# Attention scores evicted two heads at a time, block maxima joined by a TensorE transposition, and a new written-out order

## The chip, the core and the metric

The kernel runs on one core of one Trainium2 chip. The metric is device time in microseconds (us) from start to end of one launch; lower is better. The engines are named as the profile names them: PE (TensorE, with PEld for its weight loads), DVE (VectorE), ACT (ScalarE), POOL (GpSimd) and SP (SyncE, which issues the DMAs). All arithmetic is in fp32.

## The reference

One transformer block with cross-attention: 8 sequences of 256 tokens, a context of 256 tokens for each, width 512, 16 heads of 32, hidden width 2048.

```python
x = layer_norm(hidden_states, ln1_w, ln1_b)
q = x @ q_w + q_b;  k = enc @ k_w + k_b;  v = enc @ v_w + v_b      # 16 heads of 32
scores = einsum('bhqd,bhkd->bhqk', q, k) * scale
scores = where(mask, scores, finfo.min)
attn = softmax(scores, axis=-1)
out = einsum('bhqk,bhkd->bhqd', attn, v) @ cproj_w + cproj_b
hidden = out + residual
y = layer_norm(hidden, ln2_w, ln2_b)
y = gelu(y @ fc_w + fc_b, approximate=True) @ proj_w + proj_b
return hidden + y
```

## The kernel before

**Staging.** The batch is cut into two groups of four sequences. For each group the kernel makes q, k and v, then attention, then the output projection with the second layer norm, then the MLP (`fc`, gelu, `proj`). All large products are made block-wise with seven products in place of eight (`quad`, L848), in the MLP twice nested; the sums and differences of blocks that this needs are made by DVE and POOL. Products of each `quad` go to three PSUM banks X, Y and W.

**Attention.** `attention` (L1384) walks over 32 units. A unit `ghb` is group g, a set hg of four heads, and sequence b: unit 023 is group 0, heads 8 to 11, sequence 3. `scores` (L1009) does the following for a unit:

- `s`: eight matmuls make the transposed scores, keys on the partitions (two halves kc of 128 keys) and 256 queries along the row, for four heads j. A head's contraction is 32 deep, so four matmuls, one for each head, run in the four row strips of the array at once ("32\*128" in the profile). Each head has a PSUM bank of its own.
- `ev` (L1018, by the helper at L619): ACT copies them to SBUF tiles `pr` and adds the mask as a bias for each partition: eight instructions of 128x256.
- `mx` (L1022): two DVE instructions transpose blocks of 32x32 and take the maximum of each block row, over the keys of one strip of 32 partitions. `mt` (L1026) turns the result, three ACT copies `mc` (L1029) bring strips 1 to 3 to the partitions of strip 0, and `fold` (L1030) takes the maximum over eight blocks.
- `md` and `mm`: the 32x32 result goes to DRAM and comes back as one row of 1024 maxima, laid out on all 128 partitions.
- `less` (L1047 on POOL in two instructions, L1042 on DVE in one): subtracts them, and `exp` (L1050) follows on ACT.

`attend` (L1057) then makes the sums of the exponentials and the product with v, 16 matmuls with 32 columns each in four column strips ("128\*32"), divides on DVE (`r` at L1073 to L1076) and writes the head outputs (`att`, by the helper at L630).

**Order.** Nothing is scheduled at build time. Every step is recorded as a named operation (`T.op`), and `Order.run` (L94) puts them out in the order of the words of `PROGRAM`; a letter behind a colon picks the engine where there is a choice (V for DVE, A for ACT, G for POOL). Each engine works through its own instructions in that order and waits at semaphores where it needs another engine. `PLACES` gives each tile its slot; in PSUM there are three banks W and five banks C.

```python
BANKS = {"W": 3, "C": 5}
...
sb = [Buf(f"s{u}_{j}", "C", 2) for j in range(4)]
```

Of the kernel before, what the change touches and what calls it, by code (L numbers as in the profile page):

```python
# [43 lines left out]
class Order:  # L44
# [49 lines left out]
    def run(self):  # L94
# [20 lines left out]
        for o in order:  # L115
            for b in o.bufs:
                if b.slot is None and b.name in where:
                    w = where[b.name]
                    b.home = w[0] if not w[0].isdigit() else b.kind
                    b.slot = int(w.lstrip("WC"))  # L120
# [4 lines left out]
cq0_00_1 cq0_00_0 vw00 cq0_01_1 cq0_01_0 rows8 rows7 cq0_10_0 turn_c0_00 rows0 turn_c0_10 c0_00:A cq0_10_1 c0_10:V  # L125
cq0_11_0 small v0_0_P1 cq0_11_1 kw01 turn_c0_11 fw0_01_0 v0_1_P1 c0_11:A vw11 rows5 turn_c0_01 rows2 turn_c0_30
vw10 c0_01:A turn_c0_20 mk c0_30:A c0t1:G c0_20:V v0_0_t1:A vw01 turn_c0_21 v0_1_t1:V turn_c0_31 fw0_11_1 k0_0_P2
c0_21:V rows3 c0_31:V c0t2:V kw10 k0_1_P2 rows4 kw11 c0t3:V kw00 rows6 v0_0_P2 vws1:V fw0_10_0 c0t4:V fw0_00_0
v0_1_P2 vws2:V fw0_00_1 kws1:V xt0_3 rows1 k0_1_P1 fw0_10_1 kws2:V mk~1 xt0_0 kws3:V fw0_11_0 v0_0_c11 fw0i1_1:G
v0_1_P6 fw1_00_1 vws4:V xt0_2 fw0i1_2:V fw0s3:V fw1_00_0 k0_0_P1 v0_1_t2:A xt0_6 fw0i7_1:V fw1_10_0 v0_1_c11  # L130
fw0i7_2:G fw1_11_0 cols v0_1_P5 cols~1 qw10 k0_0_t1:V qw11 fw0i7_4:V fw0s1:V xt0_1 v0_0_P6 v0_1_t3:A fw1_11_1
fw0s2:V fw1_10_1 xt0_5 k0_0_P6 fw0i6_3:V xt0_4 k0_1_t1:V fw0i6_1:G cb fw0i5_1:G v0_1_P3 k0_0_t2:V kws4:G fw0i1_4:V
k0_1_P6 stats_x0_30 fw0i1_3:G fw1i1_1:V stats_x0_00 fw0i6_2:G k0_0_P5 fw1i1_3:V k0_1_t2:A xt0_7 v0_0_t2:V fw1i1_2:G
fw0_01_1 stats_x0_10 fw1i1_4:G fcd0_1_True aggr_x0_30 k0_1_P5 fw1i4_1:V qw01 aggr_x0_00 stats_x0_01 fw1i4_2:G
fw1_01_0 fw0i6_4:V fcd0_6_False stats_x0_11 k0_1_P7 k0_1_t3:A fw1_01_1 aggr_x0_01 fw0i7_3:V k0_0_t3:A eps_x0_0
fcd0_7_False stats_x0_31 pow_x0_0 qw00 aggr_x0_31 k0_1_P3 fw1i4_4:G k0_1_c22 fcd0_7_True fw0i5_2:G aggr_x0_11
fcd0_5_False nb_x0_0 k0_0_c11 fw0i5_4:G norm_x0_01:A v0_0_P5 aggr_x0_10 k0_1_c11 fw0i2_1:G norm_x0_00:A fw1i4_3:V
k0_1_c12:A fw0i2_2:V k0_0_P7 eps_x0_1 eps_x0_3 fw0i5_3:V stats_x0_20 pow_x0_3 stats_x0_21 pow_x0_1 k0_0_P3 nb_x0_3
nb_x0_1 fw0i2_3:V norm_x0_31:A aggr_x0_20 aggr_x0_21 eps_x0_2 fw0i2_4:V norm_x0_10:A pow_x0_2 k0_0_c22 fcd0_2_True
k0_1_P4 v0_0_t3:V fw1i2_1:G fcd1_4_True k0_0_c12:A fcd0_6_True norm_x0_11:A nb_x0_2 fw0s4:V kd0_0_11 k0_0_P4  # L140
fcd1_1_True vws3:V norm_x0_20:A fcd0_3_False fw1i2_2:V fcd0_5_True norm_x0_21:A qws1:V turn_x0_10 norm_x0_30:A
fw1i2_4:G k0_0_c21 turn_x0_00 x0_10:A turn_x0_20 turn_x0_30 x0_20:A v0_0_P3 x0_30:V qws3:G xt1_2 cb1_02 x0_00:V
v0_1_c12:A fw0i3_1:V turn_x0_31 fw1i2_3:V turn_x0_11 fw0i3_2:V x0_31:A turn_x0_21 fw1s1:V turn_x0_01 q0_0_P1
x0_01:A qws2:G v0_0_c12:V fcd1_5_False x0_21:A k0_1_c21 fcd1_2_True fw1i5_3:G cb1_20 x0_11:A q0_0_P2 cb1_03
q0_0_t1:A x0t1:V q0_1_P1 fw0i3_3:V q0_0_c11 x0t2:V s000 fw0i3_4:V x0t3:V q0_0_P6 ev000_11 ev000_31 fw1s3:V xt1_3
ev000_10 ev000_01 cb1_12 q0_0_P7 x0t4:V kd0_0_21 q0_0_t2:A fcd1_7_False q0_1_t1:A fw1s2:V ev000_21 ev000_00 q0_0_P5
mx000_0 fw1s4:G fcd1_6_False cb1_10 q0_1_P6 q0_0_t3:A ev000_30 q0_0_c22 ev000_20 stats_x1_10 fcd1_3_False q0_1_P2
fw1i3_3:V fw1i5_1:V q0_1_t2:V fw1i5_2:G mx000_1 q0_0_P4 fw1i6_1:G qws4:G q0_1_c11 q0_1_P5 q0_0_c21 fw1i5_4:V mt000
fw0i4_3:G fcd1_5_True mc000_3 mc000_2 s020 cb1_13 mc000_1 fw1i6_3:G fold000 cb1_00 fw1i7_1:V q0_0_P3 md000 ev020_30
fw0i4_1:V ev020_21 fw1i7_2:V cb1_23 ev020_00 fw0i4_2:G cb1_21 ev020_10 fw1i7_4:G ev020_20 cb1_01 q0_1_P7 ev020_01  # L150
cb1_11 fw1i3_1:G ev020_31 q0_0_c12:A mx020_1 fw1i6_2:G ev020_11 s002 fw1i3_2:G mm000 mx020_0 fw0i4_4:G v0_1_P7
fw1i7_3:G mt020 stats_x1_11 mc020_2 mc020_3 fw1i6_4:G q0_1_t3:V ev002_30 ev002_11 fw1i3_4:G aggr_x1_10 aggr_x1_11
v0_0_P7 mc020_1 q0_1_c22 ev002_01 ev002_00 fold020 ev002_10 eps_x1_1 md020 ev002_31 pow_x1_1 ev002_20 q0_1_P3
fcd1_7_True v0_0_c22 ev002_21 cb1_31 nb_x1_1 mx002_0 less000_1:G mm020 s022 mx002_1 cb1_33 cb1_22 v0_0_P4 ev022_20
cT1_10 cb1_32 ev022_30 cT1_00 ev022_11 cb1_30 less000_0:G ev022_31 mt002 v0_1_c22 ev022_21 q0_1_P4 ev022_00 mx022_1
# [24 lines left out]
av012 xb1_10 ev023_00 less001_1:G ev023_01 mt003 v1_0_t3:V ev023_31 ev023_21 mc003_2 v1_0_P7 mc003_3 r012 ev023_20  # L180
ev023_30 mc003_1 ev023_10 att012 ev023_11 xT1_20 s011 exp001_0 fold003 mx023_0 md003 v1_1_P2 ev011_00 mm021
# [330 lines left out]
def tile_xattn_block(  # L512
# [154 lines left out]
    def col(i):  # L667
        return cols.t[:, i : i + 1]
# [830 lines left out]
```

## Time and profile before

| | |
|---|---|
| runs timed | 662.54, 662.69, 663.8 us; median 662.69 |
| profiled execution | span 662.0 us from first to last instruction, 11469 instructions |
| PE busy | 654.6 us, 99% of the span |
| PEld busy | 490.0 us, 74% |
| DVE busy | 585.7 us, 88% |
| POOL busy | 374.8 us, 57% |
| ACT busy | 342.4 us, 52% |
| DMA moved | 144.84 MB, mean 219 GB/s |

The profile is of an execution of its own, and no total time is listed for it beside its span. The span begins at the first instruction and ends at the last, so it lies 0.7 us under the median of the runs; that difference is what lies around it. In a row of the profile, "idle before" is the time in which the engine stood still just ahead of the instructions, with what ended it. An fp32 matmul of the program appears as two records, a transposition as one. Records of PE overlap, since matmuls are pipelined: the price of one is the distance between the starts of neighbours, not its own length.

### The profile page before, as it was taken

Reading aid. Unit: us, or ns where it says so; the run is one execution under the profiler, and the core shown is the slowest. Engines: PE = TensorE matmul, PEld = TensorE weight load, DVE = VectorE, ACT = ScalarE, POOL = GpSimd, SP = SyncE. Lnnn points to the kernel's source line nnn. Section 1 sums busy time; section 2 is a strip of 40 time slices with the busy share of each in tenths; the row PEclk is TensorE's granted clock in tenths of the full one; section 3 lists DMA queues with packets and bytes.
Section 4 is the critical chain, followed back from the end, with each engine's and each line's share of the span. In section 5 each row is a group of like instructions: output and inputs, shape, how many; then the busy total and the mean of one; then the engine's idle time right before and its main releaser. Section 6 shows DMA issues by size and latency. Waiting matters only on the chain.

```text
span 662.0 us, 11469 instructions
## 1 busy us (share of the span) xinstructions
PE 654.6 (99%) x3925; PEld 490.0 (74%) x3925; DVE 585.7 (88%) x980; ACT 342.4 (52%) x702; POOL 374.8 (57%) x340
## 2 busy tenths in 40 slices
PE   8999999999999999999999999999999999999997
PEld 7746554477544776777688888888888888888887
DVE  2998799999999999999999998997789787998775
ACT  2046479799999899866995572030020013930000
POOL 1262773646888997699958774423535217720260
PEclk9999999999999999999999999999999999999999
DMA  8999888786574467886878698889978779359366
GB/s 250 311 356 307 211 197 291 267 255 125 144 241 161 144 202 234 263 268 197 266 249 273 198 235 225 289 269 230 195 193 241 190 201 242 93 142 240 106 141 111
DMA packets 206586, 144.84 MB, mean 219 GB/s; under 512 B 117008, under 2 KB 166976, under 8 KB 206528
## 3 DMA queue, kind: packets, MB, share of 16 engines
q1 hardware_dynamic: 206528, 144.11, 76.8%
q8 instruction: 31, 0.51, 0.3%
q14 instruction: 27, 0.22, 0.1%
HBM read 104.10 MB, written 39.98 MB: 218 GB/s over the span
## 4 chain that ended last, share of the span: by engine, by line
PE 92%; DVE 5%; ACT 1%; DMA 1%; issue 0%; SPq 0%; POOL 0%; DVEq 0%; ACTq 0%
PE pd_X L639 15%; PE fc_X L639 14%; PE fc_W L639 8%; PE av L639 7%; PE pd_W L639 7%; PE s L639 4%; PE o_X L639 4%; PE q_X L639 4%; PE k_X L639 4%; PE v_X L639 4%; PE pd_Y L639 4%; PE fc_Y L639 4%; PE q_W L639 2%; PE k_W L639 2%; PE v_W L639 2%; PE o_W L639 2%
## 5 line engine op out<-in xcount | busy, mean ns | idle before, releaser
L1047 POOL TENSOR_TENSOR pr<-pr,mm 128x512 f32<-128x512 f32 x84 | 110.4, 1346 | 22.8 <-DMA mm<-md 9.2
L619 ACT ACTIVATE pr<-s,cols 128x256 f32<-128x256 f32 x256 | 104.5, 482 | 21.8 <-PE s L639 15.8
L1022 DVE TRANSPOSE_TENSOR_REDUCE mx<-pr 128x32 f32<-128x1024 f32 x64 | 77.6, 1223 | 3.3 <-ACT pr L619 3.3
L1227 ACT ACTIVATE h<-h,cols 128x256 f32<-128x256 f32 x128 | 54.1, 498 | 36.7 <-DVE h L630 36.6
L1050 ACT ACTIVATE pr<-pr 128x1024 f32<-128x1024 f32 x64 | 66.9, 1069 | 3.4 <-POOL pr L1047 2.8
L630 DVE TENSOR_TENSOR h<-fc_X,h 128x512 f32<-128x512 f32 x80 | 52.8, 679 | 6.2 <-PE fc_X L639 5.5
L630 DVE TENSOR_TENSOR h<-fc_W,h 128x512 f32<-128x512 f32 x48 | 32.0, 679 | 5.8 <-PE fc_W L639 5.3
L639 PE MATMUL av<-pr,ones 128*32 128x256 f32 x512 | 34.2, 384 | 0.7 <-ACT pr L1050 0.6
L1029 ACT COPY mx<-mx 32x64 f32<-32x64 f32 x96 | 23.1, 243 | 19.8 <-DVE mx L1026 15.8
L1042 DVE TENSOR_TENSOR pr<-pr,mm 128x1024 f32<-128x1024 f32 x22 | 30.8, 1407 | 0.0
L628 POOL TENSOR_TENSOR z1i<-h,z1i 128x512 f32<-128x512 f32 x4 | 5.7, 1440 | 40.4 <-PE pd_X L639 40.4
L639 PEld LDWEIGHTS av<-pr,ones 128*32 128x32 f32 x512 | 14.1, 109 | 18.5 <-issue 6.7
L630 POOL TENSOR_TENSOR h<-h,fl 128x512 f32<-128x512 f32 x9 | 11.5, 1295 | 24.6 <-DVE fl L630 15.0
L639 PE MATMUL fc_W<-y1i,fl 128*128 128x256 f32 x100 | 24.6, 380 | 0.0
L639 PE MATMUL fc_X<-y1i,fl 128*128 128x256 f32 x88 | 21.6, 381 | 0.0
L639 PEld LDWEIGHTS fc_W<-y1i,fl 128*128 128x128 f32 x100 | 18.9, 190 | 2.9 <-DVE h L630 0.3
L639 PE MATMUL pd_W<-z0i,pl 128*128 128x256 f32 x88 | 20.6, 379 | 0.0
L1030 DVE TENSOR_REDUCE mx<-mx 32x32 f32<-32x256 f32 x32 | 18.4, 574 | 1.4 <-ACT mx L1029 1.3
L639 PE MATMUL pd_X<-z0i,pl 128*128 128x256 f32 x80 | 18.9, 379 | 0.0
L606 ACT COPY fl<-fc_X 128x512 f32<-128x512 f32 x6 | 3.5, 580 | 29.5 <-PE fc_X L639 29.2
L639 PEld LDWEIGHTS fc_X<-y1i,fl 128*128 128x128 f32 x88 | 16.6, 190 | 2.6 <-ACT h L606 0.2
L639 PEld LDWEIGHTS pd_W<-z0i,pl 128*128 128x128 f32 x88 | 16.7, 190 | 2.3
(595 smaller groups left out, 1815.6 us busy)
## 6 DMA issues: line engine op xcount, KB each, us to landing
mm<-md SPq DMA_DIRECT2D x32, 512.0 KB, 5.1
pl<-prd SPq DMA_DIRECT2D x47, 256.0 KB, 4.2
fl<-fcd SPq DMA_DIRECT2D x41, 256.0 KB, 4.0
fl<-prd SPq DMA_DIRECT2D x24, 256.0 KB, 3.8
fw<-in_L_xattn_fc_w_dram SPq DMA_DIRECT2D x16, 256.0 KB, 4.9
pw<-in_L_xattn_proj_w_dram SPq DMA_DIRECT2D x32, 128.0 KB, 3.6
hid<-in_x_dram SPq DMA_DIRECT2D x8, 512.0 KB, 4.8
hd<-hid SPq DMA_DIRECT2D x8, 512.0 KB, 3.4
```

The costliest lines, as they stand in the source:

```text
L606: (nc.scalar.copy if e == "ACT" else nc.vector.tensor_copy)(to(), of_())
L619: lambda e: nc.scalar.activation(to(), of_(), AF.Identity, bias=bias(), scale=1.0))
L628: nc.gpsimd.tensor_tensor(to()[:, ts(k, 512)], in0()[:, ts(k, 512)], in1()[:, ts(k, 512)], op)
L630: E[e].tensor_tensor(to(), in0(), in1(), op)
L639: nc.tensor.matmul(o(), l(), r(), start=first, stop=True, skip_group_check=True)
L1022: T.op(f"mx{u}_{h}", [("DVE", 1.126)], [(pr[h], None)], [(mx, [h])], lambda e, h=h: nc.vector.tensor_reduce(tile_of(mx)[:, 0:64].rearrange ...
L1029: lambda e, a=a: nc.scalar.copy(tile_of(mx)[0:32, 64 + 64 * a : 128 + 64 * a], tile_of(mx)[32 * a : 32 * a + 32, 64:128]))
L1030: T.op(f"fold{u}", [("DVE", 0.38)], [(mx, [2, 3, 4, 5])], [(mx, [6])], lambda e: nc.vector.tensor_reduce(tile_of(mx)[0:32, 320:352], tile_ ...
L1042: nc.vector.tensor_tensor(p_, p_, m_[:, :, None, :].to_broadcast([P, 2, 2, S]), ALU.subtract)
L1047: E[e].tensor_tensor(p_, p_, at(M, j)[:, None, :].to_broadcast([P, 2, S]), ALU.subtract)
L1050: lambda e, h=h: nc.scalar.activation(tile_of(pr[h]), tile_of(pr[h]), AF.Exp), table="exp")
L1227: lambda e, f=f, b=b, c=c: nc.scalar.activation(at(h[f][b], c), at(h[f][b], c), AF.Gelu_apprx_tanh, bias=col(c_fcb + f * 4 + c), scale=1.0 ...
```

## The change

- **Eviction.** Two heads share a tile of two PSUM banks. One ACT instruction evicts both of them for one half of the keys: four instructions of 128x512 for a unit in place of eight of 128x256. The tile `pr` is laid out by key half first, then by head.
- **Maxima.** `mt` and the three copies `mc` are gone. `km` on DVE joins the two key halves, `pt` on PE transposes 96 columns of `mx` into a PSUM tile `tm`, and `fold` on DVE takes the maximum over four strips, reading PSUM.
- **PSUM.** The fixed banks W and C become four pairs of banks, and any half of a pair can serve as W or C.
- **`less`.** The same subtraction, with operands in the new layout.
- **Order.** `PROGRAM` and `PLACES` are written anew as a whole; some steps change engine.

```diff
-SLOTS = {"Q": (45, 1024), "P": (36, 512), "H": (14, 256), "sm": (10, 32), "mx": (3, 352)}
-BANKS = {"W": 3, "C": 5}
+SLOTS = {"Q": (45, 1024), "P": (36, 512), "H": (14, 256), "sm": (10, 32), "mx": (3, 128)}
+BANKS = ("W", "C", "D")
...
 PROGRAM = """
-cq0_00_1 cq0_00_0 vw00 cq0_01_1 cq0_01_0 rows8 rows7 cq0_10_0 turn_c0_00 rows0 turn_c0_10 c0_00:A cq0_10_1 c0_10:V
+cq0_00_1 cq0_00_0 small vw00 turn_c0_00 c0_00:A cq0_10_1 cq0_01_0 mk cq0_01_1 cq0_10_0 kw00 cq0_11_1 vw11 cq0_11_0
...
+            elif b.kind == "D":
+                b.t = banks.tile([P, 1024], F32, tag=f"B{b.slot // 2}", name=b.name)
+                twos[b.slot // 2] = None
             else:
-                b.t = banks.tile([P, 512], F32, tag=f"{b.home}{b.slot}", name=b.name)
+                s, k = divmod(b.slot, 2)
+                if twos.get(s) is None:
+                    twos[s] = banks.tile([P, 1024], F32, tag=f"B{s}", name=b.name)
+                b.t = twos[s][:, ts(k, 512)]
...
-        sb = [Buf(f"s{u}_{j}", "C", 2) for j in range(4)]
+        sb = [Buf(f"s{u}_{h}", "D", 4) for h in range(2)]
...
-            for j in range(4):
-                copy(f"ev{u}_{j}{kc}", (pr[j // 2], [2 * (j % 2) + kc]), (sb[j], [kc]), lambda j=j, kc=kc: at(pr[j // 2], 2 * (j % 2) + kc),
-                     lambda j=j, kc=kc: at(sb[j], kc), 256, lambda kc=kc: col(2 * (4 * g + b) + kc))
+            for h in range(2):
+                T.op(f"ev{u}_{h}{kc}", [("ACT", 0.62)], [(sb[h], [kc, 2 + kc]), (cols, None)], [(pr[h], [2 * kc, 2 * kc + 1])],
+                     lambda e, h=h, kc=kc: nc.scalar.activation(
+                         at(pr[h], kc, 1, 512).rearrange("p (i q) -> p i q", i=2),
+                         tile_of(sb[h]).rearrange("p (i k q) -> p i k q", i=2, k=2)[:, :, kc, :],
+                         AF.Identity, bias=col(2 * (4 * g + b) + kc), scale=1.0))
...
-        T.op(f"mt{u}", [("DVE", 0.15)], [(mx, [0, 1])], [(mx, [2])], lambda e: nc.vector.transpose(tile_of(mx)[:, 64:128], tile_of(mx)[:, 0:64]))
-        for a in range(1, 4):
-            T.op(f"mc{u}_{a}", [("ACT", 0.2)], [(mx, [2])], [(mx, [2 + a])],
-                 lambda e, a=a: nc.scalar.copy(tile_of(mx)[0:32, 64 + 64 * a : 128 + 64 * a], tile_of(mx)[32 * a : 32 * a + 32, 64:128]))
-        T.op(f"fold{u}", [("DVE", 0.38)], [(mx, [2, 3, 4, 5])], [(mx, [6])], lambda e: nc.vector.tensor_reduce(
-            tile_of(mx)[0:32, 320:352], tile_of(mx)[0:32, 64:320].rearrange("p (m c) -> p c m", c=32), axis=mybir.AxisListType.X, op=ALU.max))
+        T.op(f"km{u}", [("DVE", 0.13)], [(mx, [0, 1])], [(mx, [2])], lambda e: nc.vector.tensor_reduce(
+            tile_of(mx)[:, 64:96], tile_of(mx)[:, 0:64].rearrange("p (k n) -> p n k", k=2), axis=mybir.AxisListType.X, op=ALU.max))
+        tm = Buf(f"tm{u}", "C")
+        T.op(f"pt{u}", [("PE", 0.11)], [(mx, [0, 1, 2]), (ident, None)], [(tm, None)],
+             lambda e: nc.tensor.transpose(tile_of(tm)[0:96, 0:P], tile_of(mx)[:, 0:96], ident.t), mode="full")
+        T.op(f"fold{u}", [("DVE", 0.2)], [(tm, None)], [(mx, [3])], lambda e: nc.vector.tensor_reduce(
+            tile_of(mx)[64:96, 96:128], tile_of(tm)[64:96, 0:P].rearrange("p (a r) -> p r a", a=4), axis=mybir.AxisListType.X, op=ALU.max))
```

How the new order moves instructions is shown at unit 023. A tile keeps its name until its slot is given away; behind the change a pair of PSUM banks keeps the name of the tile that first took it, so that a name such as `tm023` or `first` stands on products of other steps too.

On PE, the stretch from the second product of unit 023 to the next unit's column work, before the change (`s023` are the four heads' scores, `v1_0_X` and `v1_1_X` products of the value projection, `av012` the attention product of an earlier unit):

```order
L639 MATMUL v1_0_X_1372<-vws1_333,c1t1_1003 128x256 x4
L639 MATMUL v1_1_X_1392<-vws1_333,c1t1_1003 128x256 x4
L639 MATMUL s023_0_1578<-q0_0_22_730,ku023_1484 128x256
L639 MATMUL s023_1_1580<-q0_0_22_730,ku023_1484 128x256
L639 MATMUL s023_2_1582<-q0_0_22_730,ku023_1484 128x256
L639 MATMUL s023_3_1584<-q0_0_22_730,ku023_1484 128x256
...
L639 MATMUL av012_1596<-pr012_0_1123,ones_91 32x256 x2
```

On PE after the change, the stretch in which the transpositions of units 003 and 023 stand (rows at L1012; `s011` are scores of a later unit):

```order
L1012 MATMUL tm003_1494<-ident_64,mx003_1418 96x128
L617 MATMUL first_71<-vws4_397,c1_11_969 128x256 x4
L617 MATMUL s011_0_1515<-v0_0_11_321,ku011_1010 128x256 x2
L617 MATMUL s011_1_1518<-v0_0_11_321,ku011_1010 128x256 x2
...
L617 MATMUL v1_0_X_1271<-vws3_290,c1t3_991 128x256 x4
L1012 MATMUL tm023_1547<-ident_64,mx023_1505 96x128
L617 MATMUL tm023_1547<-vw01_268,c1_10_916 128x256 x4
```

Nothing of the maxima stood on PE before; now two transpositions stand between the projections, with one set of scores and two products between them.

On DVE, the maxima of unit 023 before the change (`mx023` maxima, `x1_..` transposed inputs of group 1):

```order
L1022 TENSOR_REDUCE mx023_1658<-pr023_0_1614 128x2x2x8
L630 TENSOR_TENSOR xt1_1_1174<-v1_1_Y_1661,xt1_1_1174 128x512
L1022 TENSOR_REDUCE mx023_1658<-pr023_1_1621 128x2x2x8
L1026 STREAM_TRANSPOSE mx023_1658<-mx023_1658 128x64
L758 STREAM_TRANSPOSE x1_11_1693<-xb1_2_1500 128x512
L1022 TENSOR_REDUCE mx011_1696<-pr011_1_1670 128x2x2x8
L630 TENSOR_TENSOR vw11_261<-v1_0_W_1625,vw11_261 128x512
L1022 TENSOR_REDUCE mx011_1696<-pr011_0_1666 128x2x2x8
L1026 STREAM_TRANSPOSE mx011_1696<-mx011_1696 128x64
L758 STREAM_TRANSPOSE x1_00_1746<-xb1_1_1594 128x512
L1030 TENSOR_REDUCE mx023_1658<-mx023_1658 32x32
```

On DVE after the change, from the fold of unit 003 (which needs PE's `tm003`) to that of unit 023 (which needs `tm023`); the row at L1008 is `km`:

```order
L1013 TENSOR_REDUCE mx003_1418<-tm003_1494 32x32
L1055 TENSOR_REDUCE rc032_1527<-first_71 128x8
L1057 RECIPROCAL rc032_1527<-rc032_1527 128x8
L1058 STREAM_TRANSPOSE r032_1530<-rc032_1527 128x256
L1004 TENSOR_REDUCE mx023_1505<-pr023_1_1496 128x2x16
L608 TENSOR_TENSOR att0_11_1159<-first_71,r032_1530 128x256
L584 COPY vws1_303<-first_71 128x512
L1008 TENSOR_REDUCE mx023_1505<-mx023_1505 128x32
L608 TENSOR_TENSOR v1_0_21_1407<-v1_0_X_1271,v1_0_21_1407 128x512
L1013 TENSOR_REDUCE mx023_1505<-tm023_1547 32x32
```

Before, the unit's last maximum and its fold lie seven DVE instructions apart, one of them `mt`, and ACT's copies fall into that time. Now `km` and three others lie between them, and PE's transposition falls between `km` and the fold: it stands at a fixed place in PE's own row.

Counted down the whole order, PE's matmuls are 2015 before and 2047 after, the difference being the 32 transpositions. Changes of PE between full, row-strip and column-strip work are 98 before and 93 after. `less` is done 22 times by DVE and 42 times by POOL before, 18 and 46 times after; of the other DVE instructions of 128x1024 nine go, and POOL has 20 more of 128x512 beside those of `less`. The first three loads and the last group of products, transpositions and stores are of the same kinds in both.

More of the change, by code (lines that the diff above doesn't have):

```diff
@@ L117, in run @@
                 if b.slot is None and b.name in where:
-                    w = where[b.name]
-                    b.home = w[0] if not w[0].isdigit() else b.kind
-                    b.slot = int(w.lstrip("WC"))
+                    b.slot = int(where[b.name])
         return order
 PROGRAM = """
-cq0_00_1 cq0_00_0 vw00 cq0_01_1 cq0_01_0 rows8 rows7 cq0_10_0 turn_c0_00 rows0 turn_c0_10 c0_00:A cq0_10_1 c0_10:V
-cq0_11_0 small v0_0_P1 cq0_11_1 kw01 turn_c0_11 fw0_01_0 v0_1_P1 c0_11:A vw11 rows5 turn_c0_01 rows2 turn_c0_30
@@ L127 @@
[L127 to L131, printed above, removed]
@@ new lines @@
+stats_x0_00 v0_1_P6 aggr_x0_00 v0_0_P6 kw10 stats_x0_11 c0t3:G aggr_x0_01 rows1 cols cols~1 kw11 k0_0_P2 k0_0_t1:A
+fw1_11_0 fw0_10_0 aggr_x0_11 stats_x0_10 aggr_x0_10 xt0_4 k0_0_c11 fw1_01_1 v0_1_t2:A stats_x0_20 eps_x0_1 k0_1_P2
+v0_1_P5 v0_1_t3:A c0t4:V xt0_5 kws1:G vws4:G xt0_7 v0_0_c11 fw0_11_1 kws2:G eps_x0_0 fw0_10_1 pow_x0_1 k0_1_t1:A
+nb_x0_1 k0_0_P6 v0_0_t2:A k0_0_t2:A aggr_x0_20 pow_x0_0 stats_x0_21 k0_1_P6 nb_x0_0 norm_x0_01:A fw0_11_0 k0_1_t2:A
+qw01 fw0_00_0 kd0_0_11 kws3:G fw0i1_3:G norm_x0_00:A fw0s1:V qw11 norm_x0_10:A k0_1_c11 v0_0_P5 stats_x0_31 cb1_00
@@ L462 @@
[L462 to L465 removed]
+cq0_00=8 cq0_10=60 cq0_01=82 cq0_11=86 ps_cols=5 ps_c0_00=0 c0_00=2 ps_c0_10=1 ps_c0_20=5 c0_10=50 ps_c0_30=2
@@ L646, in tile_xattn_block @@
     nc.vector.memset(warm, 1.0)
-    first = banks.tile([P, 512], F32, tag="W0", name="first")
+    twos[0] = banks.tile([P, 1024], F32, tag="B0", name="first")
+    first = twos[0]
     def small(n):
@@ L1038, in less @@
             def less(e, h=h):
+                m_ = at(M, 2 * h, 2)
                 if e == "DVE":
-                    p_ = tile_of(pr[h]).rearrange("p (i k q) -> p i k q", i=2, k=2)
-                    m_ = tile_of(M)[:, 512 * h : 512 * h + 512].rearrange("p (i q) -> p i q", i=2)
-                    nc.vector.tensor_tensor(p_, p_, m_[:, :, None, :].to_broadcast([P, 2, 2, S]), ALU.subtract)
+                    p_ = tile_of(pr[h]).rearrange("p (k n) -> p k n", k=2)
+                    nc.vector.tensor_tensor(p_, p_, m_[:, None, :].to_broadcast([P, 2, 512]), ALU.subtract)
                     return
-                for i in range(2):
-                    j = 2 * h + i
-                    p_ = at(pr[h], i, 1, 512).rearrange("p (k q) -> p k q", k=2)
-                    E[e].tensor_tensor(p_, p_, at(M, j)[:, None, :].to_broadcast([P, 2, S]), ALU.subtract)
+                for k in range(2):
+                    p_ = at(pr[h], k, 1, 512)
+                    E[e].tensor_tensor(p_, p_, m_, ALU.subtract)
             T.op(f"less{u}_{h}", [("POOL", 2.448), ("DVE", 1.16)], [(pr[h], None), (M, None)], [(pr[h], None)], less, lock=True, pieces=2)
```

654 lines of the change are left out of this document (314 added, 340 removed).

## The prediction

> **What bounds the kernel now.** First the page: shares of the engines, granted clock, and the chain that ended last.
>
> ```profile
> span 662.0 us, 11469 instructions
> ...
> PE 654.6 (99%) x3925; PEld 490.0 (74%) x3925; DVE 585.7 (88%) x980; ACT 342.4 (52%) x702; POOL 374.8 (57%) x340
> PEclk9999999999999999999999999999999999999999
> PE 92%; DVE 5%; ACT 1%; DMA 1%; issue 0%; SPq 0%; POOL 0%; DVEq 0%; ACTq 0%
> ```
>
> PE is busy 654.6 of 662.0 us, its clock is nowhere cut, and 92% of the chain is PE's own. A busy share says little by itself, since the records overlap. So next the chain in order of time (start, length, engine and product, records).
>
> ```profile
> 50.54 1.75 PE ps_x L726 x16
> ...
> 179.41 1.91 PE q_X L639 x4
> 181.32 1.73 PE q_Y L639 x4
> ...
> 433.23 6.91 PE pd_X L639 x32
> ```
>
> Thirty-two records take 6.91 us, 0.216 each, one behind the other without a gap, and the pieces of other stages keep the same distance (four wide records, twice as long, in 1.73 us). PE streams. Sixteen transpositions take 1.75 us, 0.109 each. Those four take 1.73 us behind work of the same shape (`q_Y`) and 1.91 us behind attention's column strips (`q_X`): a change of shape costs 0.18 us.
>
> Then the busy time by stretch (length, then PE, PEld, DVE, ACT, POOL, granted clock, DMA) and PE's waits.
>
> ```profile
> 100.00:200.00 100.00, 99.88 (x790) 57.09 (x790) 94.60 (x157) 94.02 (x197) 63.16 (x45) 1.00 0.75 220
> 200.00:300.00 100.00, 97.85 (x839) 68.68 (x838) 97.90 (x177) 84.72 (x177) 87.27 (x79) 1.00 0.66 211
> 600.00:662.00 62.00, 58.64 (x283) 51.48 (x281) 47.14 (x81) 0.00 (x0) 14.93 (x12) 1.00 0.62 143
> ```
>
> ```profile
> PE ps_y L726 <- DVE att L630: 1.2, 2, 1.0
> PE first L651 <- DVE warm L646: 1.0, 1, 1.0
> PE av L639 <- ACT pr L1050: 0.6, 1, 0.6
> PE v_X L639 <- DMA vw<-in_L_xattn_v_w_dram: 0.5, 1, 0.5
> PE fc_Y L639 <- DVE h L630: 0.2, 1, 0.2
> PE ps_c L726 <- DMA cq<-in_ctx_dram: 0.2, 1, 0.2
> ```
>
> The last column is the longest single wait. Of PE's 7.4 us of idle time, 1.7 lie at the start (the rows of `first`, `v_X`, `ps_c`), 3.4 at the end, where the last stores land, and some 2.1 between 200 and 300 us, where DVE has 97.9 of 100 us to do. Start and end keep their kinds of work, so I count nothing there. Only the last can be won, by the rows 2.0 us: `ps_y` 1.2, `av` 0.6, `fc_Y` 0.2. The kernel's time is the sum of what PE does, plus little.
>
> **The change part by part.** The rows of what is removed, and of the nearest things to what is added:
>
> ```profile
> L619 ACT ACTIVATE pr<-s,cols 128x256 f32<-128x256 f32 x256 | 104.5, 482 | 21.8 <-PE s L639 15.8 <-PE av L639 2.7 <-issue 1.8
> L1029 ACT COPY mx<-mx 32x64 f32<-32x64 f32 x96 | 23.1, 243 | 19.8 <-DVE mx L1026 15.8 <-issue 1.6 <-ACT pr L1050 0.7
> L611 ACT ACTIVATE q<-q_X,cols 128x512 f32<-128x512 f32 x5 | 3.3, 686 | 1.8 <-issue 1.5 <-PE q_X L639 0.3
> ...
> L1022 DVE TRANSPOSE_TENSOR_REDUCE mx<-pr 128x32 f32<-128x1024 f32 x64 | 77.6, 1223 | 3.3 <-ACT pr L619 3.3
> L1042 DVE TENSOR_TENSOR pr<-pr,mm 128x1024 f32<-128x1024 f32 x22 | 30.8, 1407 | 0.0
> L1030 DVE TENSOR_REDUCE mx<-mx 32x32 f32<-32x256 f32 x32 | 18.4, 574 | 1.4 <-ACT mx L1029 1.3
> L1076 DVE STREAM_TRANSPOSE r<-rc 128x256 f32<-128x256 f32 x32 | 14.3, 445 | 1.1
> L1073 DVE TRANSPOSE_TENSOR_REDUCE rc<-av 128x8 f32<-128x256 f32 x32 | 13.6, 426 | 2.5 <-PE av L639 2.4
> L630 DVE TENSOR_TENSOR att<-av,r 128x256 f32<-128x256 f32 x32 | 13.1, 414 | 0.6
> ...
> L1026 DVE STREAM_TRANSPOSE mx<-mx 128x64 f32<-128x64 f32 x32 | 7.4, 234 | 0.6
> L1075 DVE RECIPROCAL rc<-rc 128x8 f32<-128x8 f32 x32 | 6.5, 203 | 1.1
> L606 DVE COPY c<-ps_c 128x512 f32<-128x512 f32 x4 | 2.7, 686 | 11.4 <-PE ps_c L726 11.4
> ...
> L1047 POOL TENSOR_TENSOR pr<-pr,mm 128x512 f32<-128x512 f32 x84 | 110.4, 1346 | 22.8 <-DMA mm<-md 9.2 <-ACT pr L619 7.9 <-DMA kd<-k 3.0
> ```
>
> *Eviction, on ACT.* The 256 evictions keep ACT busy for 104.5 us: 0.408 each, less than the 0.482 of one alone, since neighbours overlap. An eviction of 512 elements with a bias is listed at 0.686. Without any overlap 128 of them take 87.8 us; with the same 0.074 of overlap, 78.3. ACT saves 17 to 26 us, not the 36 that 2 x 0.482 - 0.686 would suggest. The copies `mc` save 23.1 more. ACT is busy for 52%, and PE waited for it for 0.6 us in all: 40 to 49 us off ACT are worth at most that 0.6. What covers them is PE's own row; were PE not full, they would show. Reading two banks at once is not in the trace; even at twice the price ACT would stay under 60%.
>
> *Maxima, on DVE.* `mt` (7.4 us) and the old fold (18.4 us) go. `km` and the new fold are not in the trace. Each is small, so 0.2 us (reciprocal) is the lower bound and 0.57 (old fold, twice the elements of the new) the upper. I take 0.2 for `km`, nearest to `mt`, and 0.35 for the fold, between the reciprocal and `rc`, which also reads PSUM: together 17.6 us, 8 us less than before. Four `less` leave DVE, 5.6 us more. POOL takes these as 8 instructions and 20 others of its size, some 38 us at 1.346: it goes from 57% to about 62%, still with room. The nine 128x1024 instructions that leave DVE take another 10 us or so, by the price of `mx`, of the same size. DVE comes down by some 25 us, mostly in the attention stretch. It is not what bounds, so this counts only through the 1.2 + 0.2 us that PE waits for it.
>
> *Transpositions, on PE.* These are new work on the full engine: 32 x 0.109 = **+3.5 us**, all on the path, since PE runs its matmuls in order. They need 128 rows and 96 columns, the full array. Were a narrow output cheaper, the price could be no lower than 0.08 (96/128 of it); with weights that arrive late and a shape change on both sides it is 0.109 + 2 x 0.18.
>
> *Order, on PE.* Changes of shape fall from 98 to 93 with the transpositions counted as full work: 5 x 0.18 = **-0.9 us**. The number of other matmuls does not change, so PE gains nothing else.
>
> *Waits that may go.* With less to do on DVE between 200 and 300 us I take `ps_y`'s wait as gone: **-1.2 us**. Bounds: 0 and the whole 2.0.
>
> *Waits that may come.* `pt` makes PE wait for `km` on DVE, at 32 places, and behind it in PE's row stand projections, scores and attention products for everything else. At unit 023 the margin can be read off the rows of the order shown: from the fold of 003 to `km` of 023, DVE does 0.35 + 0.426 + 0.203 + 0.445 + 1.223 + 0.414 + 0.686 + 0.2 = 3.9 us; PE has two products of 1.73, one set of scores and its changes of shape, the scores about 1.1.
>
> ```profile
> 126.79 1.15 PE L639 MATMUL s<-q,ku 32*128 32x256 f32 x16
> 127.87 1.07 PE L639 MATMUL av<-pr,ones 128*32 128x256 f32 x16
> ```
>
> (Start to start, 1.08 us.) That is 4.6 to 4.7 us: a margin of some 0.7 us. Any DVE step that comes late by more stops PE. I take five places late by 0.2 us, the `fc_Y` wait: **+1.0 us**. Bounds: 0, and 32 x 0.2 = 6.4.
>
> *The sum.* +3.5 - 0.9 - 1.2 + 1.0 = +2.4 us on the span of 662.0, so 664.4; with the 0.7 us between span and median, **665.1 us**. A measurement of this kernel tells about 0.2% (1.3 us; its runs lie 1.3 us apart): 661.4 to 664.0 is no change.
>
> *A rule that speaks against reading PE as full.* The Trainium skill, "Trainium Kernel Development and Optimization", section Performance Expectations, calls the matmul busy share a bad measure and the share of weight loads a good one. By it PE stands at 74% and 3.5 us would be lost in the free quarter, so that only the other terms were left: the first rival below. The trace does not bear this out here: 32 records at 0.216 us each leave no gap to fill, whatever the weight loads do.
>
> **The rivals.**
>
> *PE has room* (faster; 0.08). The transpositions slip into holes that the records don't show, and the rest stays: -0.9 - 1.2 = -2.1, 660.6 us. For it: PEld is busy for only 490.0 us. Against it: the spacing of the records. It decides if the neighbours of a `pt` keep their old distance.
>
> *The maxima free the path* (no change; 0.30). All 2.0 us of waits go and no `pt` waits: +3.5 - 0.9 - 2.0 = +0.6, 663.3 us. For it: DVE loses some 25 us and ACT over 40. Against it: 32 new meeting points with an engine that is still busy for over 80%. [...]
>
> *DVE is late at the transpositions* (much slower; 0.12). If every `pt` waits 0.2 us, the sum is +3.5 - 0.9 + 6.4 = +9.0, 671.7 us. It decides where the margin of 0.7 us is used up at most places. For it: DVE has 94.6 and 97.9 us in 100 between 100 and 300 us. Against it: DVE gets lighter, and the `ps_y` row shows PE waiting for DVE just twice before.
>
> *The new order stumbles elsewhere*: `less` moves to POOL, where a half unit takes 2.7 us in place of DVE's 1.4, so `exp` and `av` come later. PE waited 0.6 us once for this; the cost is within the range of the likeliest case.
>
> **How the numbers follow.** The likeliest case, 665.1, gets 0.50; the others 0.08, 0.30 and 0.12. Its own range is 664.1 (no new waits) to 668.1 (new waits at 4.0). For 8 in 10 the range runs from **661.8**, below the no-change rival and short of PE with room, to **669.0**, which leaves out the greater part of the case of late DVE. Faster by over 0.2%: 0.09, the first rival and a start that happens to be shorter. Within 0.2%: 0.31. Slower: 0.60.
>
> **What would show it.** In the profile after: 32 `pt` records with a neighbour 0.109 us on, and 0.109 more between the products around them; PE's busy time up by 2 to 4 us; ACT down by 40 to 49 us, DVE by some 25, POOL up by some 38, with no gain of time from any of these; the `ps_y` wait gone; a new row of PE waiting at `tm` for DVE `mx`, of about 1 us in all. The prediction is wrong if the span falls under 660.7, if the `tm` row is over 3 us, or if PE's records keep their distance around a transposition.

## The result, and the profile after

The changed kernel takes 779.65 us (median of four runs, 777.2 to 781.32). The kernel before takes 663.25 us beside it (662.54 to 663.96). The ratio is 1.174, with a 95% interval of 1.171 to 1.178: 116 us slower, where 665.1 was forecast and the range ended at 669.0.

The page of the kernel after, its span, engines, granted clock and chain:

```profile
span 777.1 us, 11317 instructions
...
PE 687.8 (89%) x3957; PEld 498.8 (64%) x3957; DVE 568.5 (73%) x951; ACT 302.1 (39%) x482; POOL 429.6 (55%) x378
PEclk9999998999998899999999899999999999999999
PE 30%; DVE 7%; DMA 2%; issue 2%; POOL 1%; ACT 0%; SPq 0%; POOLq 0%; DVEq 0%
```

PE had been idle for 7.4 us of its span; now it is idle for 777.1 - 687.8 = 89.3 us. The last line cannot be laid beside the 92% of before: this chain could be followed back only to 441.5 us, so that its shares add up to 42% of the span in all, and 30 of these 42 are PE's. Every other engine is less busy as a share than before, so none of them has become the bound. Everyone waits.

The busy time by stretch (length, then PE, PEld, DVE, ACT, POOL, granted clock, DMA share, GB/s) says where:

```profile
100.00:200.00 100.00, 88.07 (x641) 51.90 (x644) 73.74 (x138) 55.75 (x80) 59.05 (x49) 0.97 0.66 175
200.00:300.00 100.00, 86.66 (x635) 52.08 (x631) 75.78 (x122) 59.95 (x86) 69.88 (x54) 0.93 0.39 117
...
400.00:500.00 100.00, 88.31 (x451) 70.70 (x450) 80.63 (x118) 45.39 (x84) 51.45 (x46) 0.97 0.61 193
...
600.00:700.00 100.00, 88.59 (x383) 71.81 (x382) 76.53 (x114) 27.68 (x64) 43.24 (x36) 0.98 0.59 153
```

It is everywhere. The stretches from 500 us on hold the MLP's last products and no attention, and PE still stands idle for 11.4 us of the 100 from 600 to 700. So the loss cannot sit in the transpositions or in the scores' eviction alone, which belong to attention. PE's waits, costliest first (total, times, longest single wait):

```profile
PE av L617 <- DVE h L608: 7.8, 10, 1.5
PE fc_Y L617 <- DVE h L608: 5.7, 5, 3.1
PE fc_W L617 <- DVE h L608: 4.5, 4, 2.3
PE ps_c L617 <- DVE rc L1055: 4.2, 2, 4.0
PE q_X L617 <- ACT ows L589: 4.1, 1, 4.1
PE first L617 <- DVE k L608: 3.8, 1, 3.8
PE o_W L617 <- DVE h L608: 2.7, 2, 1.9
PE tm L1012 <- DVE mx L1008: 2.5, 3, 1.7
```

The row that was forecast, `tm` waiting for DVE's `mx`, is there with 2.5 us, under the bound of 3 us. It comes eighth. Ahead of it are rows that make no sense as data: a projection that writes `ps_c` waits for the softmax's `rc`, an attention product that writes `q_X` for an eviction into `ows`. (A pair of banks keeps the name of its first user, so the left-hand names say which pair is written, not what for.) The longest of the DVE waits, in order of time:

```profile
125.90 1.88 PE L617 MATMUL first<-c1t,kws 128*128 128x512 f32 x4
...
131.16 0.44 DVE L1055 TRANSPOSE_TENSOR_REDUCE rc<-ps_c 128x8 f32<-128x256 f32 x1
131.63 0.20 DVE L1057 RECIPROCAL rc<-rc 128x8 f32<-128x8 f32 x1
131.75 2.90 PE L617 MATMUL ps_c<-c1t,xt 128*128 128x512 f32 x3 [3.97 <-DVE rc L1055]
```

PE stops for 3.97 us until DVE has read `ps_c`, and then writes `ps_c`. That looks like a bank that is still in use. In the built program DVE reads columns 768 to 1023 of this tile and PE writes columns 0 to 511. They are two different banks. The tile is a pair, and the wait is between its halves. The 4.1 us of `q_X` are of the same kind: ACT reads columns 0 to 511 there, and PE writes from column 768 on.

### The profile page after: what moved, and what is told of

It reads as the page before. It is cut to its first block, busy times and chain, and to the rows that moved or that the text cites. A ratio compares the mean times of both kernels' runs of the same rounds, so it can differ in the third digit from the quotient of the medians.

```text
span 777.1 us, 11317 instructions
## 1 busy us (share of the span) xinstructions
PE 687.8 (89%) x3957; PEld 498.8 (64%) x3957; DVE 568.5 (73%) x951; ACT 302.1 (39%) x482; POOL 429.6 (55%) x378
## 5 line engine op out<-in xcount | busy, mean ns | idle before, releaser
L998 ACT ACTIVATE pr<-s,cols 128x512 f32<-128x512 f32 x128 | 80.2, 686 | 80.2 <-PE s L617 59.9
L608 DVE TENSOR_TENSOR h<-av,h 128x512 f32<-128x512 f32 x88 | 58.8, 682 | 11.6 <-PE av L617 11.1
L617 PE MATMUL av<-z1i,pl 128*128 128x256 f32 x144 | 33.7, 380 | 1.4 <-issue 1.4
L617 PEld LDWEIGHTS av<-z1i,pl 128*128 128x128 f32 x144 | 27.1, 190 | 5.9 <-issue 1.9
L608 DVE TENSOR_TENSOR h<-fc_W,h 128x512 f32<-128x512 f32 x27 | 18.3, 679 | 13.4 <-PE fc_W L617 13.2
L608 DVE TENSOR_TENSOR po<-av,po 128x256 f32<-128x256 f32 x33 | 13.7, 414 | 14.6 <-PE av L617 14.0
L606 POOL TENSOR_TENSOR z1i<-z1t,z1i 128x512 f32<-128x512 f32 x10 | 14.4, 1470 | 10.5 <-DVE z1i L608 9.4
L608 DVE TENSOR_TENSOR h<-fc_Y,h 128x512 f32<-128x512 f32 x24 | 16.0, 678 | 4.6 <-PE fc_Y L617 4.6
L606 POOL TENSOR_TENSOR z1i<-h,z1i 128x512 f32<-128x512 f32 x12 | 16.8, 1425 | 3.8 <-issue 2.5
L597 ACT ACTIVATE att<-att,cols 128x512 f32<-128x512 f32 x16 | 11.4, 718 | 15.2 <-DVE att L608 15.2
L786 POOL TENSOR_TENSOR rs_y<-rs_y,neg_half 128x2 f32<-128x2 f32 x8 | 8.1, 1016 | 14.8 <-DVE rs_y L783 9.8
L617 PE MATMUL av<-y1i,fl 128*128 128x256 f32 x56 | 14.4, 383 | 1.6 <-DVE fl L608 0.9
L1058 DVE STREAM_TRANSPOSE r<-rc 128x256 f32<-128x256 f32 x32 | 14.3, 446 | 1.1
```

Of the source, the lines that this page charges most:

```text
L597: lambda e: nc.scalar.activation(to(), of_(), AF.Identity, bias=bias(), scale=1.0))
L606: nc.gpsimd.tensor_tensor(to()[:, ts(k, 512)], in0()[:, ts(k, 512)], in1()[:, ts(k, 512)], op)
L608: E[e].tensor_tensor(to(), in0(), in1(), op)
L617: nc.tensor.matmul(o(), l(), r(), start=first, stop=True, skip_group_check=True)
L786: lambda e, rs=rs: nc.gpsimd.tensor_tensor(tile_of(rs)[:, 2:4], tile_of(rs)[:, 0:2], neg_half[:, 0:2], ALU.pow), lock=True)
L998: lambda e, h=h, kc=kc: nc.scalar.activation(at(pr[h], kc, 1, 512).rearrange("p (i q) -> p i q", i=2), tile_of(sb[h]).rearrange("p (i k q) ...
```

## Theories

**Theory 1.** The two banks of a pair are one tile, and the program orders accesses of different engines by tile. So an access to one bank waits for another engine's access to the other bank. In the built program of the kernel after, 131 of PE's waits are for an instruction that reads only the other bank of the pair PE writes (104 on DVE, 27 on ACT); in the kernel before, where each bank is a tile, at most one. **Theory 2:** the order written anew puts work at the wrong places. **Theory 3:** the transposition, waiting for DVE, holds up PE's row. **Rival 5:** the eviction over two banks costs by holding both.

## The experiments

**All banks apart** (`banks_apart`). Order, slots and transposition stay. The edit in short (the old branch stays in the file and is never taken):

```diff
-                twos[s] = banks.tile([P, 1024], F32, tag=f"B{s}", name=b.name)
-            b.t = twos[s][:, ts(k, 512)]
+            b.t = banks.tile([P, 512], F32, tag=f"A{b.slot}", name=b.name)
...
-                b.t = banks.tile([P, 1024], F32, tag=f"B{b.slot // 2}", name=b.name)
+                b.t = [banks.tile([P, 512], F32, tag=f"A{b.slot + i}", ...) for i in range(2)]
...
+                for i in range(2):
+                    nc.scalar.activation(at(pr[h], 2 * kc + i), bank_of(sb[h], i)[:, ts(kc, 256)], ...)
```

> Changed kernel in all but its PSUM tiles: each of the eight banks is a tile of its own, and a score bank pair is two tiles that ScalarE empties with two 128x256 instructions where the changed kernel has one over both banks. The written-out order, the slots and the transposition stay. Theory 1 (the two banks of a pair are one tile, so that an access to the one bank waits for an access of another engine to the other bank): about 666 us (662 to 672), near the prediction's sum of 665.1, with TensorE's waits back from some 107 us to under 15. Theory 2 (the new written-out order has TensorE's work at the wrong places): stays at 765 to 785. Theory 3 (the transposition on TensorE waits for VectorE and holds the queue up): stays at 765 to 785.

Measured: 668.9 us (10 runs), ratio to the kernel before 1.006 (1.003 to 1.009). Of the 116 us, 111 are gone with the written-out order and the transposition in place. Theories 2 and 3 fall as causes of the loss. The page and two of the stretches, to be laid beside those above:

```profile
span 666.2 us, 11406 instructions
...
PE 654.7 (98%) x3957; PEld 496.0 (74%) x3957; DVE 560.9 (84%) x951; ACT 319.1 (48%) x610; POOL 426.0 (64%) x378
```

```profile
200.00:300.00 100.00, 99.18 (x849) 70.89 (x848) 94.96 (x172) 75.77 (x146) 80.63 (x75) 1.00 0.68 213
...
400.00:500.00 100.00, 100.00 (x464) 87.69 (x463) 80.59 (x132) 23.94 (x45) 55.86 (x45) 1.00 0.88 230
```

PE is full again, idle for 666.2 - 654.7 = 11.5 us, and the clock is whole. (What the expectation calls some 107 us of waits in the changed kernel is 89.3 us of idle time on its page.)

**The kernel before, with its banks in pairs** (`before_paired`). The converse: one thing is added to a kernel that has nothing else of the change.

```diff
+    twos = [banks.tile([P, 1024], F32, tag=f"B{s}", name=f"two{s}") for s in range(4)]
...
-                b.t = banks.tile([P, 512], F32, tag=f"{b.home}{b.slot}", name=b.name)
+                s, k = divmod(b.slot + (3 if b.home == "C" else 0), 2)
+                b.t = twos[s][:, ts(k, 512)]
```

> The kernel before, with its order, its evictions and its ScalarE copies of maxima as they are; only its eight PSUM banks are now four tiles of two banks (W0 with W1, W2 with C0, C1 with C2, C3 with C4). Theory 1 (banks of one tile wait for each other): slower by as much as the change or more, 730 to 800 us. Theories 2 and 3 (the new order, the transposition): neither is in this kernel, so 662 to 666 us as before.

Measured: 738.15 us, ratio 1.108 (1.103 to 1.114). With pairs the tuned order loses 74 us, without any other part of the change.

```profile
span 736.3 us, 11466 instructions
...
PE 677.4 (92%) x3925; PEld 491.5 (67%) x3925; DVE 592.2 (80%) x980; ACT 344.8 (47%) x702; POOL 374.3 (51%) x340
```

**Its control** (`before_kept`). The same edit with eight tiles of 512 columns, one for each bank, made once.

> Control for the paired form of the kernel before: eight tiles of one bank each, made once and kept for all uses of the bank, where the kernel before makes a new tile for each use. Theory 1: the size of the tile decides, not that it is kept, so 662 to 667 us. Rival 1b (a tile that is kept over its uses loses the wait on its release and gets worse ones): as slow as the paired form, over 700 us.

Measured: 663.5 us (one run). In it, a tile that is kept over its uses costs nothing; that it spans two banks is what costs.

**Half of the pairs** (`half_paired`, banks 4 to 7) **and the other half** (`low_paired`, banks 0 to 3).

> As the run with all banks apart, but only banks 0 to 3 are tiles of their own; banks 4 to 7 stay two pairs of the changed kernel, which hold 53 of 61 score pairs with the one eviction over both. In the built program 43 of TensorE's waits are for an instruction that reads only the other bank of a pair, against 131 in the changed kernel and none with all apart. Theory 1: by that share, a third of the loss is left, about 703 us (685 to 725). Theories 2 and 3: 765 to 785.

> The counterpart of the half-paired run: banks 0 to 3 are the changed kernel's two pairs, banks 4 to 7 tiles of their own, so that only 8 of the 61 score pairs keep the one eviction over two banks. Theory 1 (the pair as one tile costs, whoever uses it): 93 of TensorE's waits are then for the other bank of a pair, against 43 in the half-paired run that lost 34 us against banks apart, and the two losses add up to the changed kernel's 111 us: 735 to 755 us. Rival 5 (the eviction over two banks is what costs, by holding both banks): 8 of 61 evictions, so 670 to 685 us.

Measured: 703.03 and 746.09 us. Over all banks apart (668.9) that is 34.1 and 77.2 us, together 111.3; both halves at once, the changed kernel, lose 779.65 - 668.9 = 110.8. The losses add up. (The two were timed on different chips; by the ratios to the kernel before, timed beside each, the losses are 5.0% and 11.6%, together 16.5%, against 16.8% for both halves.) They follow the count of waits on the other bank, 43 and 93 (0.79 and 0.83 us for each), not the evictions over two banks. The row of these in the second kernel:

```profile
L1013 ACT ACTIVATE pr<-s,cols 128x512 f32<-128x512 f32 x16 | 10.5, 690 | 9.2 <-POOL pw0i L616 5.2 <-PE s L625 3.5 <-PE o_W L625 0.6
```

It keeps 16 of the 128, for 8 of the 64 score pairs (the expectations' 53 and 8 of 61 should read 56 and 8 of 64), and loses the more. In the paired kernel before, such a wait cost less: 74 us for about 150 in its built program, 0.5 us each.

**Pairs, with one eviction for each bank** (`pairs_split`).

```diff
-                     lambda e, h=h, kc=kc: nc.scalar.activation(
-                         at(pr[h], kc, 1, 512)..., tile_of(sb[h])...[:, :, kc, :], ...))
+                     lambda e, h=h, kc=kc: [nc.scalar.activation(
+                         at(pr[h], 2 * kc + i), at(sb[h], 2 * i + kc), ...) for i in range(2)])
```

> The changed kernel with its pairs of banks as one tile each; only the score eviction is again two ScalarE instructions of 128x256, one for each bank, where the changed kernel has one of 128x512 over both. Theory 1 (the pair as one tile): no gain, 775 to 790 us. Rival 5 (the instruction over two banks costs, by holding or reading both at once): most of the 111 us come back, 665 to 700 us.

Measured: 780.36 us, as slow as the changed kernel. Rival 5 falls. The eviction's price is on ACT alone; its row in this kernel (128x256, 256 times), and then in the kernel after (128x512, 128 times; below it the row of `km`), with total and mean ns:

```profile
L998 ACT ACTIVATE pr<-s,cols 128x256 f32<-128x256 f32 x256 | 100.0, 487 | 74.6 <-PE s L617 56.2 <-issue 8.6 <-POOL pw0i L608 4.9
```

```profile
L998 ACT ACTIVATE pr<-s,cols 128x512 f32<-128x512 f32 x128 | 80.2, 686 | 80.2 <-PE s L617 59.9 <-issue 9.1 <-POOL pw0i L608 5.5
...
L1008 DVE TENSOR_REDUCE mx<-mx 128x32 f32<-128x64 f32 x32 | 6.6, 209 | 0.4
```

The one instruction saves some 20 us of ACT's time and none of the kernel's.

The rest asks about the terms of the prediction's sum, in the kernel with banks apart.

**Five transpositions for one** (`apart_five_turns`), timed beside the kernel with banks apart once more (`banks_apart_again`, 670.16 us, ratio 1.007, 1.004 to 1.011).

```diff
-             lambda e: nc.tensor.transpose(tile_of(tm)[0:96, 0:P], ...), mode="full")
+             lambda e: [nc.tensor.transpose(tile_of(tm)[0:96, 0:P], ...) for _ in range(5)], mode="full")
```

> The kernel with all banks apart once more, as the measure on this chip for the two runs beside it, which change one thing each in it: 666 to 671 us.

> All banks apart, and each of the 32 transpositions of maxima on TensorE is issued five times, to the same place. The prediction has them on TensorE's row at 0.109 us each, with nothing to hide them: 128 more make 14.0 us (12 to 16) over banks apart, so that the 32 of the change cost 3.5. Rival (TensorE has room beside its waits, the transposition is free): within 3 us of banks apart.

Measured: 680.57 us, ratio 1.023 (1.019 to 1.026). 128 more transpositions cost 10.4 us; by the two intervals 7 to 14. That is 0.08 us each (0.05 to 0.11): far from nothing, with the 0.109 of the sum at the upper end. In the profiles PE's busy time is 668.6 us, 13.9 more than with banks apart (654.7) and 11.1 more than in the second profile of that kernel (657.5). PE is full, and new work on it shows. The four extra transpositions stand behind one of their own kind, so what the change of shape adds to the first is not in this price.

In that second profile (span 672.1 us) PE also waits at the transposition, which no row of the first shows:

```profile
PE tm L1031 <- DVE att L616: 2.5, 2, 2.4
```

**ScalarE's copies in place of the transposition** (`apart_copies`): `mt`, three copies and the old fold, at the places of `km`, `pt` and `fold`.

> All banks apart, and the maxima of a unit brought together as in the kernel before: VectorE turns the 64 maxima, three ScalarE copies take the place of TensorE's transposition at its place in the order, and VectorE folds 256 values. Prediction's price of the transposition (32 x 0.109 us on TensorE's row, here 3.5 us): 3 to 4 us faster than the run with banks apart, about 664 to 665 us where that was 668 to 669. Rival (TensorE has room for it, the residue above the kernel before is elsewhere): the same within 1 us.

Measured: 685.28 us, ratio 1.029 (1.022 to 1.037): 15 to 16 us slower than with the transposition (670.16 and 668.9, on other chips), where 3 to 4 us faster was expected. Both expectations miss. The fold's row, here and with the transposition:

```profile
L1033 DVE TENSOR_REDUCE mx<-mx 32x32 f32<-32x256 f32 x32 | 18.6, 581 | 14.8 <-ACT mx L1031 14.8
```

```profile
L1032 DVE TENSOR_REDUCE mx<-tm 32x32 f32<-32x128 f32 x32 | 9.2, 289 | 8.8 <-PE tm L1031 8.1
```

DVE now stands idle for 14.8 us until ScalarE's copies are done, where it waited 8.1 us for PE, and the folds take 9 us longer in sum. PE now waits for ScalarE's evictions and exponentials, which it does nowhere in the first profile with the transposition; the longest row:

```profile
PE av L625 <- ACT pr L1052: 3.4, 3, 2.1
```

So in the places that this order gives the step, the way through ScalarE holds up other work, and the exchange does not price the transposition alone. How the 15 to 16 us divide was not taken apart.

**The end of the order** (`apart_tail`, `apart_copies_tail`, `apart_two_queues`). In the kernel before, 3.4 us of the span lie behind the end of PE's last matmul; with banks apart it is 7.0, from 659.2 to 666.2 (the expectations below count both from the last matmul's start). The end in order of time, with banks apart and then in the kernel before:

```profile
650.28 8.65 SPq L585 DMA_DIRECT2D out_dram<-tq  x13
...
657.27 1.95 PE L625 MATMUL pd_V<-pl,z1i 128*128 128x128 f32 x16
659.03 0.73 SPq L585 DMA_DIRECT2D out_dram<-pl  x1
...
659.80 1.34 SPq L585 DMA_DIRECT2D out_dram<-tq  x2
661.24 0.54 SPq L585 DMA_DIRECT2D out_dram<-ot  x1
661.90 0.57 SPq L585 DMA_DIRECT2D out_dram<-pl  x1
```

```profile
645.57 10.16 SPq L599 DMA_DIRECT2D out_dram<-tq  x12
656.69 1.95 PE L639 MATMUL pd_V<-fl,z1i 128*128 128x128 f32 x16
656.72 2.78 SPq L599 DMA_DIRECT2D out_dram<-ot  x3
```

Before, the stores of `tq` were issued by 655.7 us. With banks apart, in the new order, they go on to 661.1, and the last ones stand among and behind them. Two mends were tried. In the first the last additions go from GpSimd to VectorE, and three stores stand earlier:

```diff
...
-tr1_33 out1_31:G pl14_3 ... tr1_11 out1_11:G pd14_P5
+tr1_33 out1_31:V pl14_3 ... tr1_11 out1_11:V pd14_P5
...
-turn_o11 out1_10:G so1_10 ... so1_03 ot00 ot11 turn_o10 so1_02 st00 so1_32 ot10 so1_12 z1i4_4:G
+turn_o11 out1_10:V so1_10 ... so1_03 so1_02 so1_32 so1_12 ot00 ot11 turn_o10 st00 ot10 z1i4_4:G
```

> All banks apart with the transposition, and the end of the order mended: the five last additions of output tiles run on VectorE where GpSimd has them, and three stores of these tiles stand ahead of the last additions, as in the kernel before. In the profile of banks apart 7.3 us of the span lie behind the last matmul, 3.6 in the kernel before; SyncE waits 7.8 us for GpSimd's additions there and then issues eleven stores in a row. If that tail is the new order's own price: 3 to 4 us faster than banks apart, 664.5 to 666 us, tail 3.5 to 4.5 us. Rival (the tail is set by the transfers' bytes, not by when the stores are issued): the same within 1 us.

> Both of the former at once: banks apart, ScalarE's copies in place of the transposition, and the mended end. If the transposition and the tail are what the new order loses against the kernel before, the two savings add up: 7 us under banks apart, 661 to 663 us, no slower than the kernel before (662.5 to 664) and perhaps 1 to 2 us faster for its fewer changes of tile shape. Rival (other losses in the new order): 664 to 667 us.

Measured: 674.61 us, ratio 1.014 (1.006 to 1.021), and with the copies 685.54 us, as without the mend. It does not help: the first interval overlaps that of banks apart (1.003 to 1.009), and its middle lies above. The end in order of time, of the first of the two:

```profile
654.88 12.12 SPq L585 DMA_DIRECT2D out_dram<-tq  x15
662.51 1.95 PE L625 MATMUL pd_V<-pl,z1i 128*128 128x128 f32 x16
...
668.34 0.40 SPq L585 DMA_DIRECT2D out_dram<-pl  x1
```

All 15 stores that are left now stand in a row from 654.9 us on, and the tail is 672.3 - 664.5 = 7.8 us, 0.8 longer than with banks apart. In the second mend eight of the stores go to ScalarE's queue:

```diff
+                        if g and c in (1, 3):
+                            T.op(f"so{g}_{c}{a}", [("ACT", 0.47)], src_, [], lambda e, c=c, a=a: nc.scalar.dma_start(...))
```

> All banks apart, and eight of the sixteen last stores of turned output tiles are issued by ScalarE, which is idle there, not by SyncE, where they stand in one row with the rest. In the profile of banks apart SyncE is held by GpSimd's additions and then issues eleven stores of some 0.7 us each behind TensorE's end; 7.3 us of the span lie behind the last matmul, 3.6 in the kernel before. If the row of stores on SyncE is what lengthens the tail: tail 3.5 to 5 us and the time 2 to 4 us under banks apart. Rival (the last transfer itself, or GpSimd's additions, set the tail): within 1 us of banks apart, tail 6.5 to 7.5.

Measured: 668.96 us, ratio 1.005 (1.002 to 1.008), 1.2 us under the run beside it, and the intervals overlap. The tail is still 6.6 us. SyncE's longest waits in the last 15 us:

```profile
SPq L585 <- DVE tq L616: 4.2, 1, 4.2
SPq L585 <- DMA out_dram<-tq: 3.4, 1, 3.4
```

With two queues SyncE is held for 4.2 us by VectorE's `tq` and for 3.4 us by a transfer of `tq`. So the row of issues on SyncE is not what makes the tail, or not alone. Whether it goes when the `tq` stores are ready earlier was not tried, and stays open.

## Why the prediction was wrong

*What bounds the kernel now* was right: PE is full, and 128 extra transpositions on it show as 10.4 us.

*Eviction, on ACT*: right in size and worth. Forecast 78.3 to 87.8 us, measured 80.2; ACT came down by 40.3 us in all and the time did not. Reading two banks at once, which was not in the trace then, takes the listed 0.686 us.

*Maxima, on DVE*: `km` 0.209 us (forecast 0.2), `fold` 0.289 with banks apart (forecast 0.35). DVE came down by 17 us where some 25 were forecast (with banks apart by 24.8), and POOL went up by 55 where 38 were.

*Transpositions, on PE*: +3.5 us forecast, 2.6 by the five-fold run (1.7 to 3.4). *Waits at `pt`*: +1.0 us forecast; 2.5 in the row of the profile after, none in the first profile with banks apart and 2.5 in the second.

*Start and end keep their kinds of work, so I count nothing there*: wrong by some 3 us. In the kernel after, the span ends 6.7 us behind the last matmul.

```profile
768.36 2.02 PE L617 MATMUL av<-pl,z1i 128*128 128x128 f32 x16 [0.93 <-POOL z1i L606]
```

**The step that failed is "Waits that may come".** It counts the transposition as PE's only new meeting with another engine, and so bounds the new waits by 6.4 us; what came is 81.9 us more of idle time. The change also puts two PSUM banks into one tile. The text ahead of the prediction tells of that ("any half of a pair can serve"), and no term of the sum and no rival prices it. Two of its three signs of being wrong stayed quiet: the span did not fall under 660.7, and the `tm` row was not over 3 us. The pairing made 131 waits, at matmuls of every stage, and took PE's idle time from 7.4 to 89.3 us. The rest is in PE's busy time, 33.2 us more, of which the clock explains a part, by the estimate below some 15 us. The cause of the remainder was not taken apart.

None of the rivals had this mechanism. "The new order stumbles elsewhere" looks nearest, but the same order with banks apart loses only 0.6%. The forecast sum of +2.4 us (0.36%) lies within that kernel's first interval (0.3 to 0.9%) and just outside its second (0.4 to 1.1%). That it comes so near is in part luck. In the first profile the span is 4.2 us longer than before (666.2 against 662.0), and 3.6 of these lie in the tail, which the sum put at nothing; what the sum did count comes to 0.6 us there, where it had 2.4.

The Trainium skill, "PSUM — Partial Sum Buffer", section "PSUM bank collisions raise a hardware error", has two engines at different banks run side by side, and asks for semaphores by bank. By that the orderings between the two halves of a pair guarded nothing. The kernel with banks apart agrees: it does without them, with the order and the slots unchanged, at 668.9 us.

## What to carry to other kernels

When an edit merges two buffers into one tile, count the new orderings before pricing the instructions it saves: in the built program, look for waits whose two instructions touch different columns of the tile. Here one instruction over two banks saved 20 us on an engine that was half idle, and the tile that made it possible cost 111 us on the one that was full. Where a full engine's idle time grows in every stage at once, as here, look first at what all stages share (slots, queues, clock), and only then at the new step.

## What the runs showed of the hardware

A long wait costs PE more than itself. The order of time behind the 3.97 us wait, for PE alone, and the stretches around it (length, busy times, and the granted clock ahead of DMA's share):

```profile
131.75 3.63 PE L617 MATMUL ps_c<-c1t,xt 128*128 128x512 f32 x4 [3.97 <-DVE rc L1055]
135.30 1.15 PE L617 MATMUL s<-k,kw 32*128 32x256 f32 x16
```

```profile
131.70:135.00 3.30, 3.25 (x4) 1.18 (x4) 0.81 (x4) 0.00 (x0) 0.70 (x1) 0.50 0.00 0
135.00:140.00 5.00, 5.00 (x26) 2.28 (x25) 0.42 (x1) 3.52 (x5) 0.00 (x0) 0.99 0.00 0
```

Behind the wait four wide matmuls take 3.63 us, where four took 1.73 in the kernel before, at a granted clock of 0.50; then the clock is whole again. So this wait of 4 us cost nearly 6. The wait of 4.14 us at `q_X`, which ends at 242.56 us, shows the same, and for longer:

```profile
242.00:248.00 6.00, 5.44 (x56) 2.98 (x60) 4.55 (x7) 3.50 (x6) 6.00 (x3) 0.52 0.17 55
```

The Trainium skill, "TensorE: Matmul & The Clock Gate", Part 1, has the clock halved after an idle window of about 3.4 us and restored after as much work. The 3.97 us and the 3.3 us at 0.50 agree with that; the trace as a whole does so only in part. Read in steps of 1 us, it has seven stretches at 0.50 ahead of the tail, four of about 3.4 us and three of about 6.8. One of them, from 121.5 us on, follows a wait of 2.44 us. So here a wait shorter than 3.4 us was enough, and what decides it stays open.

Over the whole span the granted clock is 0.976 after, so that at most 0.024 x 777.1 = 19 us went this way. Counted only where PE is busy in those steps, it is some 15 us. Both are estimates.
